# A macaron block on one core: the first and last feed-forward tiles in seven block products, and attention values in full-height matmuls

## The chip, the cores and the metric

One core of a Trainium2 chip runs the kernel. It has a matrix engine (TensorE; PE is its matmul side, PEld its weight loads), VectorE (DVE), ScalarE (ACT), GpSimd (POOL) and SyncE (SP), which issues all DMAs here. The metric is device time in microseconds (us) of one execution, lower is better; a kernel's time is the median of its runs.

## The reference

`x` is 4 sequences of 256 tokens with 512 features, all in fp32. Three steps are added one after the other, each on the layer norm of `x` (mean and variance, no gain):

```python
x = x + 0.5 * ffn(_layernorm(x))
x = x + attn(_layernorm(x))
x = x + 0.5 * ffn(_layernorm(x))

def ffn(x):                          # same weights both times; xf is 1024 x 512
    probs = softmax(xf @ W_router.T)             # 8 experts, the best two kept and renormalized -> w
    h = einsum('td,erd->ter', xf, lora_A)        # rank 16 for each expert
    lora_out = einsum('ter,eor,te->to', h, lora_B, w) * 2.0
    return xf @ W_base.T + b_base + lora_out     # W_base is 512 x 512

def attn(x):                         # 32 query heads, 8 key/value heads, head size 128, rotary positions
    # a query sees itself and the 127 tokens before it
    return softmax(mask(q @ k.T / sqrt(128))) @ v @ wo
```

## The kernel before, in words

The 1024 tokens are 8 tiles of 128 tokens (`xt[0..7]`, in SBUF throughout), in two halves of two sequences each. The first feed-forward step (`f1`) goes by halves, the attention by units (half, group of four query heads, sequence; 32 units), the second feed-forward step (`f2`) by sequences, that is, by pairs of tiles.

**Feed-forward.** `ffn(tiles, tag, then)` returns a function that runs one step by its letter and a tile or pair number: M measures a tile (mean, variance and, on ACT, the root), X scales it, T transposes it (PE, then a copy by ACT), N is X and T, A multiplies by the router and the low-rank weights, R is the router (some 16 small DVE operations in a chain and one Exp on ACT, then POOL scales the low-rank activations), G transposes those and ACT copies them (`ht`), I adds the halved bias to `x` on POOL, and L multiplies `ht` by `lb_sb`, adds the bank times 0.5 to `xt` and calls `then` (which stores a tile or measures it for the attention).

The product with `W_base` comes in two forms. The plain one is B (L352 to 357): per tile four matmuls of 512 columns; for the last tile of all, H and K do it by halves of columns (L438 to 448). The other takes a pair of tiles as a 2x2 matrix of blocks (tokens by features), as is `W_base`, and makes seven products in place of eight: S forms the sums of token blocks on POOL (`sums_a`: s1, s2, s4 and a21 in place, in this order), W those of the weight on DVE (`sums_b`: t3, t1, t2, t4), and each product is two matmuls of 256 columns. P makes products 1 and 6, Q makes 5 and 7, C makes 2 and 3, D makes 4. P and Q also combine their banks on DVE (and one ACT copy); Y adds the rest to `xt` on POOL. In the kernel before, the first pair of `f1` and both pairs of the last half's `f2` are plain, the others by seven products.

**Values.** For each unit `values` (L747 to 777) multiplies the transposed probabilities by v. Its queries are eight blocks of 32 (times four heads); blocks 0 to 3 see the first 128 keys (`p0`), blocks 4 to 7 see parts of the first 128 (`old_p`) and of the second (`new_p`). The kernel makes four matmuls of 128 rows by 256 columns and four of 64 rows by 128 columns, the latter in turn on the lower and the upper 64 rows, into two PSUM banks (`oa`, `ob`) in an order of blocks of its own, which three ACT copies undo into `oT`.

**Order.** POOL and ACT run in the written order throughout. PE and DVE do so until three units before the end (`in_order.close()`), after which the framework orders them. The head is a written list of steps, shared by both halves of `f1` and the attention's first steps (`None`); the last units run steps of the second-last sequence's `f2` from the table `loose`; the tail is a list for the last two pairs (`f2[0]`, `f2[1]`) and the last output projection (`None`, 512 columns per matmul, L838). PSUM has four banks for `mm_bank` (products C, D, B, values, projections) and four for `score_bank` (transposes, A, P, Q, scores), each taken in turn.

Of the kernel before, what the change touches and what calls it, by code (L numbers as in the profile page):

```python
# [14 lines left out]
ALU = mybir.AluOpType  # L15
# [23 lines left out]
def macaron_kernel(  # L39
# [21 lines left out]
    def mm_bank(name):  # L61
        return ps.tile([P, 512], F32, tag="mm", bufs=4, name=name)

    def score_bank(name):
        return ps.tile([P, 512], F32, tag="s", bufs=4, name=name)
# [161 lines left out]
    rank = const.tile([P, E], F32, name="rank")  # L227
    for e in range(E):
        nc.gpsimd.memset(rank[:, e : e + 1], float(E - e))
    nc.gpsimd.tensor_scalar(half_bias, half_bias, 0.5, None, ALU.mult)  # L230


    moments = {}
# [13 lines left out]
    def scale(t, tag):  # L247
        if (tag, t) not in moments:
            measure(t, tag)
        mv, std = moments[tag, t]  # L250
        std = std or deviation(t, tag, mv)
        rstd = sb.tile([P, 1], F32, tag="rstd", bufs=4, name=f"rs_{tag}_{t}")
        nc.vector.reciprocal(rstd, std)
        xc = sb.tile([P, D], F32, tag="xc", bufs=3, name=f"xc_{tag}_{t}")
        if tag == "f1":
            shift = sb.tile([P, 1], F32, tag="shift", bufs=4, name=f"sh_{tag}_{t}")
            nc.vector.scalar_tensor_tensor(shift, mv[:, 0:1], -1.0, rstd, ALU.mult, ALU.mult)
            for cols in (slice(0, D // 2), slice(D // 2, D)) if t == 0 else (slice(0, D),):
                nc.scalar.activation(xc[:, cols], xt[t][:, cols], AF.Identity, bias=shift, scale=rstd)
        else:  # L260
            nc.vector.tensor_scalar(xc, xt[t], mv[:, 0:1], rstd, ALU.subtract, ALU.mult)
        moments[tag, t] = xc
# [49 lines left out]
    def ffn(tiles, tag, then):  # L312
# [76 lines left out]
            nc.vector.scalar_tensor_tensor(dst, bank, 0.5, other, ALU.mult, ALU.add)  # L389

        def one_six(j):
            bank = product(j, (1, 6), score_bank(f"p16_{tag}_{tiles[2 * j]}"))
            p1, u2 = temp("p1c", j)[:, lo], temp("u2", j)[:, lo]
            nc.scalar.mul(p1, bank[:, lo], 0.5)
            half_add(u2, bank[:, hi], p1)
            x0 = xt[tiles[2 * j]]
            half_add(x0[:, lo], bank[:, lo], x0[:, lo])
            state[j] = u2

        def seven_five(j):  # L400
            bank = product(j, (7, 5), score_bank(f"p75_{tag}_{tiles[2 * j]}"))
            u = temp("v1", j).rearrange("p (n f) -> p n f", n=2)
            half_add(
                u, bank.rearrange("p (n f) -> p n f", n=2),
                state.pop(j).unsqueeze(1).to_broadcast([P, 2, D // 2]),
            )
            x1 = xt[tiles[2 * j + 1]]
            half_add(x1[:, hi], bank[:, hi], x1[:, hi])
            state[j] = u

        def others(j):
            x0, x1, u = xt[tiles[2 * j]], xt[tiles[2 * j + 1]], state.pop(j)
            for x, n in ((x1[:, lo], 0), (x0[:, hi], 1), (x1[:, hi], 0)):
                nc.gpsimd.tensor_tensor(x, u[:, n], x, ALU.add)

        def two_three(j):
            po[2 * j] = product(j, (2, 3), mm_bank(f"po_{tag}_{tiles[2 * j]}"))

        def four(j):
            po[2 * j + 1] = product(j, (4,), mm_bank(f"po_{tag}_{tiles[2 * j + 1]}"))  # L420
# [9 lines left out]
        def leave(i):  # L430
            bank, t = po.pop(i), tiles[i]
            nc.tensor.matmul(  # L432
                bank, state["ht"][:, i, :], lb_sb, start=False, stop=True, skip_group_check=i // 2 in lhs
            )
            nc.vector.scalar_tensor_tensor(xt[t], bank, 0.5, xt[t], ALU.mult, ALU.add)
            then(t)

        def columns(i, cols):  # L438

            bank, t = mm_bank(f"po_{tag}_{tiles[i]}_{cols.start}"), tiles[i]  # L440
            if cols.start == 0:
                bias(t)
            part, xs = bank[:, : D // 2], xt[t][:, cols]
            for c in range(KC):
                nc.tensor.matmul(part, x_of(i, c), wb_sb[:, c, cols], start=(c == 0), stop=False)
            nc.tensor.matmul(part, state["ht"][:, i, :], lb_sb[:, cols], start=False, stop=True)
            nc.vector.scalar_tensor_tensor(xs, part, 0.5, xs, ALU.mult, ALU.add)
            nc.sync.dma_start(out=out[ts(t, P), cols], in_=xs)

        steps = {  # L450
            "M": look, "X": shape, "T": turn, "N": enter, "A": narrow, "R": shares, "G": gated,
            "S": sums, "I": biases, "P": one_six, "Q": seven_five, "Y": others, "C": two_three, "D": four,
            "B": base, "L": leave, "H": lambda i: columns(i, slice(0, D // 2)),
            "K": lambda i: columns(i, slice(D // 2, D)),
        }
        return lambda s: steps[s[0]](*(int(i) for i in s[1:]))

# [287 lines left out]
        return p0, parts  # L745

    def values(h, g, b, p0, p1):  # L747


        oT = sb.tile([HD, G, S], F32, tag="oT", bufs=4, name=f"oT_{h}_{g}_{b}")  # L750
        cols, half = ts(g % 2, HD), P // 2
        va, vb = (vS[h, g - g % 2][:, 2 * b + n, cols] for n in range(2))
        old_p, new_p = p1
        banks = [mm_bank(f"o{n}_{h}_{g}_{b}").rearrange("p (i c) -> p i c", i=2) for n in "ab"]

        def blocks(part, e, n=2):
            return part[:, e : e + n].rearrange("p e j q -> p (e j q)")

        def product(n, i, lhs, rhs, at=slice(None)):
            nc.tensor.matmul(  # L760
                banks[n][:, i, at], lhs, rhs, start=(i == 0), stop=True, skip_group_check=True
            )

        product(0, 0, va, blocks(p0, 2))
        product(1, 0, va, blocks(p0, 0))
        product(0, 1, va, blocks(old_p, 0))
        product(1, 1, vb, blocks(new_p, 2))
        for e in range(2):
            product(0, 1, vb[:half], blocks(new_p, e, 1)[:half], ts(e, P))
            product(1, 1, va[half:], blocks(old_p, 2 + e, 1)[half:], ts(e, P))  # L770
        blocks_of = oT.rearrange("p j (e q) -> p e j q", q=BLK)
        for e, n, src in ((2, 4, banks[0]), (0, 2, banks[1][:, 0]), (6, 2, banks[1][:, 1])):
            src = src.rearrange("p i c -> p (i c)") if n == 4 else src
            nc.scalar.copy(  # L774
                blocks_of[:, e : e + n], src.rearrange("p (e j q) -> p e j q", j=G, q=BLK)
            )
        return oT

# [107 lines left out]
    def attn(step):  # L886
        if step == "W":
            new = sb.tile([P, 4, 2, D // 2], F32, tag="qT", name="wbs")
            return sum_base(nc.vector, *(new[:, i] for i in range(4)))
        if step == "K":  # L890
            return sum_weights(step.lower(), *groups[0])
        if step[0] == "S":
            if not tokens:
                tokens.update(sum_tokens(0, *(nc.vector,) * 4))
            return tokens[int(step[1:])]()
        t = int(step[1:])
        if step[0] == "X":
            scale(t, "a")
        else:
            norm_attn(t, scaled=True)  # L900

    for h, order in (
# [5 lines left out]
    ):  # L908
        for step in order.split():
            (attn if h is None else halves[h])(step)  # L910
# [32 lines left out]
    def run(queue, n):  # L943
# [5 lines left out]
    loose = {  # L949
# [4 lines left out]
    }  # L954

    def fill(left, place):
# [6 lines left out]
    for u, (h, g, b) in enumerate(units):  # L963
# [4 lines left out]
        if left < 4:  # L968
            normalize(ahead[0], ahead[2])
        fill(left, 0)  # L970
        parts = []

        def turn(at=(h, g, b), pr=ahead[0]):
# [85 lines left out]
            first()  # L1059
        if left > 1:  # L1060
            exponentials(*ahead)
            if left == 2:
                nc.scalar.activation(root, eps, AF.Sqrt)
            if combine:
                combine()
            late.extend(outputs(h, g, b, oT))
# [11 lines left out]
        elif (h, g) == groups[-2] and b == BPH - 1:  # L1078
            late.append(lambda h=h, b=b: add_sums(h, b))
    f2 = [ffn(tiles(last[0], b, 1), "f2", store) for b in range(BPH)]  # L1080
    for n, order in (
        (0, "N0 N1"), (None, 0), (None, 1), (0, "A0 A1 R B0"), (1, "N0"), (0, "B1"),
        (1, "N1 A0 A1 R"), (0, "G L0 L1"), (1, "B0 G H1 L0 K1"),
    ):
        if n is None:
            out_project(*last, order, oT)
        else:
            for step in order.split():
                f2[n](step)
# [46 lines left out]
```

## Time and profile before

| | |
|---|---|
| median of 3 runs | 769.92 us (769.81 to 771.42) |
| the profiled execution | 769.25 us, of which span 767.5 us, granted clock 1.000 |
| PE busy | 759.9 us, 4198 matmul records (an fp32 matmul is two) |
| DVE, POOL, ACT busy | 550.5, 532.3, 214.3 us |
| 0 to 60 us | PE busy 56.95, DVE 41.80, POOL 44.58 us |
| 732.6 to 767.5 us (after the last values) | PE busy 31.53, DVE 15.44, POOL 6.63 us |
| matmuls of values (L760) | 512 records: 256 of 128x256, 256 of 64x128 |

A line of a timeline gives the start, the length, the engine, the line of the code, the operation, its output and inputs with their shapes, how many were merged, and in brackets the idle time ahead of it and what ended it. A record of PE lasts longer than the distance to the next one, since matmuls overlap in the pipeline.

### The profile page before, as it was taken

What the parts mean: (1) busy time and instruction counts of PE and PEld (TensorE: products, weight loads), DVE (VectorE), ACT (ScalarE), POOL (GpSimd) and SP (SyncE); (2) the same over time, 40 slices, a digit from 0 to 9 for tenths busy, and PEclk for the clock granted to TensorE, in tenths of its full rate; (3) what the DMA queues carried; (4) which work ended last, traced back from release to release, by engine and by line L of the source; (5) the groups of instructions that cost most, each with busy time, mean ns of one, the idle gap of its engine ahead of it and who ended that gap; (6) DMA issues with size and microseconds to landing.
All of it is one profiled execution on the core that took longest, in us unless ns stands there. A gap on an engine that the chain in (4) does not pass through costs nothing.

```text
span 767.5 us, 11815 instructions
## 1 busy us (share of the span) xinstructions
PE 759.9 (99%) x4198; PEld 656.4 (86%) x4198; DVE 550.5 (72%) x1332; ACT 214.3 (28%) x784; POOL 532.3 (69%) x579
## 2 busy tenths in 40 slices
PE   8999999999999999999999999999999999999998
PEld 6878888988898888988898889888898889888855
DVE  5787886858675868578667857586867867595963
ACT  5421132422223130322222232222041222223442
POOL 6877775848767585769594788768575959775802
PEclk9999999999999999999999999999999999999999
DMA  8302111304030303012120403030302111010001
GB/s 310 129 1 83 51 60 29 110 1 138 1 111 27 110 29 107 32 56 83 42 96 1 136 3 111 29 110 28 110 28 70 42 55 56 2 55 29 1 28 55
DMA packets 29483, 49.00 MB, mean 64 GB/s; under 512 B 1137, under 2 KB 10353, under 8 KB 29425
## 3 DMA queue, kind: packets, MB, share of 16 engines
q1 hardware_dynamic: 29424, 48.26, 19.0%
q8 instruction: 33, 0.54, 0.3%
q14 instruction: 26, 0.20, 0.1%
HBM read 46.15 MB, written 2.10 MB: 63 GB/s over the span
## 4 chain that ended last, share of the span: by engine, by line
PE 96%; DVE 2%; ACT 1%; DMA 0%; issue 0%; DVEq 0%; ACTq 0%
PE q L521 25%; PE y L796 24%; PE k L578 6%; PE oa L760 6%; PE v L628 6%; PE sb L693 5%; PE sa L679 4%; PE ob L760 4%; PE t L732 4%; PE po_f L357 2%; PE p_f L377 2%; PE pa_f L341 2%; PE po_f L377 2%; PE po_f L432 1%; PE pt_f L270 1%; PE y L838 1%
## 5 line engine op out<-in xcount | busy, mean ns | idle before, releaser
L480 POOL TENSOR_TENSOR qT<-ra_q,rb_q 128x512 f32<-128x512 f32 x64 | 81.4, 1274 | 104.5 <-DVE rb_q L474 104.5
L474 DVE TENSOR_TENSOR rb_q<-q,sin_sb 64x512 f32<-64x512 f32 x128 | 88.0, 688 | 1.7
L736 ACT COPY p<-t 128x512 f32<-128x512 f32 x32 | 18.8, 587 | 210.3 <-PE t L732 210.3
L724 POOL TENSOR_TENSOR probs<-probs,sm 128x512 f32<-128x512 f32 x64 | 65.2, 1041 | 14.8 <-DVE sm L721 13.7
L774 ACT COPY oT<-oa 128x512 f32<-128x512 f32 x32 | 18.8, 586 | 184.9 <-PE ob L760 184.9
L796 PE MATMUL y<-wos,oT 128*128 128x256 f32 x248 | 63.7, 379 | 0.0
L796 PE MATMUL y<-wo,oT 128*128 128x256 f32 x248 | 63.7, 379 | 0.0
L521 PE MATMUL q<-xa,wq 128*128 128x256 f32 x256 | 62.0, 385 | 0.7 <-ACT oT L774 0.7
L796 PE MATMUL y<-wo,oTs 128*128 128x256 f32 x244 | 62.6, 379 | 0.0
L760 PE MATMUL oa<-p,v 128*128 128x256 f32 (+1 forms) x256 | 60.9, 339 | 0.1
L521 PE MATMUL q<-xs,wq 128*128 128x256 f32 x256 | 60.5, 379 | 0.2 <-DVE rb_k L474 0.2
L521 PE MATMUL q<-xs,wqs 128*128 128x256 f32 x256 | 60.5, 379 | 0.0
L760 PE MATMUL ob<-p,v 128*128 128x256 f32 (+1 forms) x256 | 58.7, 338 | 0.0
L472 DVE TENSOR_TENSOR ra_q<-q,cos_sb 128x512 f32<-128x512 f32 x64 | 44.2, 691 | 19.7 <-PE q L521 7.2
L521 PEld LDWEIGHTS q<-xa,wq 128*128 128x128 f32 x256 | 47.2, 190 | 9.0 <-ACT oT L774 0.9
L521 PEld LDWEIGHTS q<-xs,wq 128*128 128x128 f32 x256 | 48.6, 190 | 7.1 <-issue 0.5
L521 PEld LDWEIGHTS q<-xs,wqs 128*128 128x128 f32 x256 | 48.6, 190 | 6.6
L796 PEld LDWEIGHTS y<-wo,oT 128*128 128x128 f32 x248 | 46.6, 190 | 6.0
L796 PEld LDWEIGHTS y<-wo,oTs 128*128 128x128 f32 x244 | 46.4, 190 | 6.3
L760 PEld LDWEIGHTS oa<-p,v 128*128 128x128 f32 (+1 forms) x256 | 39.9, 188 | 13.3 <-issue 10.6
L796 PEld LDWEIGHTS y<-wos,oT 128*128 128x128 f32 x248 | 45.8, 190 | 5.3
L715 ACT ACTIVATE probs<-probs,nm 128x32 f32<-128x32 f32 (+3 forms) x128 | 44.8, 358 | 10.8 <-DVE nm L708 6.0
(220 smaller groups left out, 1808.5 us busy)
## 6 DMA issues: line engine op xcount, KB each, us to landing
wq<-in_wq_dram SPq DMA_DIRECT2D x16, 1024.0 KB, 5.5
wo<-in_wo_dram SPq DMA_DIRECT2D x16, 1024.0 KB, 5.1
wk<-in_wk_dram SPq DMA_DIRECT2D x8, 512.0 KB, 3.5
wv<-in_wv_dram SPq DMA_DIRECT2D x8, 512.0 KB, 3.4
x<-in_x_dram SPq DMA_DIRECT2D x8, 256.0 KB, 6.7
out_dram<-x SPq DMA_DIRECT2D x7, 256.0 KB, 2.0
wb_sb<-in_w_base_dram SPq DMA_DIRECT2D x1, 1024.0 KB, 7.3
ar_sb<-in_w_ar_dram SPq DMA_DIRECT2D x1, 272.0 KB, 4.6
```

The costliest lines, as they stand in the source:

```text
L377: nc.tensor.matmul(bank[:, ts(i, D // 2)], lhs[j][m - 1][:, c, :], weights["bs"][m - 1][:, c, :], start=(m in (1, 5, 2, 4) and c == 0), st ...
L472: nc.vector.tensor_tensor(twice(a), twice(src), angle(cos_sb), ALU.mult)
L474: nc.vector.tensor_tensor(twice(b[o : o + half, :]), twice(src[i : i + half, :]), angle(sin_sb[o : o + half, :]), ALU.mult,)
L480: nc.gpsimd.tensor_tensor(dst, view(a), view(b), ALU.add)
L521: nc.tensor.matmul(bank[:, ts(j, S)], w[:, c, ts(j, HD)], x[:, c, :], start=(new and j == 0 and c == 0), stop=(c == 1), skip_group_check=True,
L578: nc.tensor.matmul(dst, w[n - 1][:, c, :], x[n - 1][:, c, :], start=(start and c == 0), stop=(c == 1), skip_group_check=True,)
L628: nc.tensor.matmul(bank[:, i, :], x[n - 1][:, c, ts(i, P)], w[n - 1][:, c, :], start=(start and i == 0 and c == 0), stop=(c == 1), skip_gr ...
L693: nc.tensor.matmul(pb[:, at : at + P + BLK], q[:, NB + m], k[:, o + m * BLK : o + m * BLK + P + BLK], start=True, stop=True,)
L715: nc.scalar.activation(pr[:, n, :keys_of], src[:, :keys_of], AF.Exp, bias=nm[:, n : n + 1], scale=scale, accum_out=sm[:, n : n + 1],)
L724: nc.gpsimd.tensor_tensor(w, w, sm[:, n : n + NB].unsqueeze(2).to_broadcast([P, NB, P]), ALU.mult)
L760: nc.tensor.matmul(banks[n][:, i, at], lhs, rhs, start=(i == 0), stop=True, skip_group_check=True)
L796: nc.tensor.matmul(py[:, ts(i, D // 2)], lhs[n - 1][:, c, :], weights["os", h, g][n - 1][:, c, :], start=(i == 0 and c == 0), stop=(c == 1 ...
```

## The change

- All pairs of tiles go by seven products. In `f1` the first pair gets S0, the products 1, 2, 6, 5, 7, 3, 4 and Y0; in the tail both pairs do. B, H and K are gone from the orders; the very last tile leaves by F, which multiplies `ht` by `lb_sb` and adds and stores it in two halves of columns.
- P, Q, C, L are cut into smaller steps: V and Z are what P and Q did on DVE; 1, 2, 3, 6 are single products; O and E are L without and with only `then`.
- The head's list is written anew. In it, W follows X3 of the first half, the halved bias (H, formerly in the setup of POOL) follows S0, I1 of the first half stands between S1 and R of the second half, and O0 O1 (the first half's) stand ahead of V0 Z0 of the second.
- X of tiles 0 and 1 is split: DVE scales the first 256 features, ACT the others.
- The Sqrt activation that loads ACT's table ahead of the tail moves from the second-last unit to the last one.
- In the last unit, L0 L1 of the second-last sequence's `f2` move from behind `values` to ahead of it.
- The tail's list is written anew, and PE and DVE follow the written order there too.
- `values` becomes three matmuls of 128 rows by 512 columns in two banks (p0; old and new parts accumulated), and two ACT copies.

```diff
-    nc.gpsimd.tensor_scalar(half_bias, half_bias, 0.5, None, ALU.mult)
...
         if tag == "f1":
...
-            for cols in (slice(0, D // 2), slice(D // 2, D)) if t == 0 else (slice(0, D),):
-                nc.scalar.activation(xc[:, cols], xt[t][:, cols], AF.Identity, bias=shift, scale=rstd)
+            cols = slice(D // 2 if t < 2 else 0, D)
+            if t < 2:
+                lo = slice(0, D // 2)
+                nc.vector.tensor_scalar(xc[:, lo], xt[t][:, lo], mv[:, 0:1], rstd, ALU.subtract, ALU.mult)
+            nc.scalar.activation(xc[:, cols], xt[t][:, cols], AF.Identity, bias=shift, scale=rstd)
...
         def one_six(j):
-            bank = product(j, (1, 6), score_bank(f"p16_{tag}_{tiles[2 * j]}"))
-            p1, u2 = temp("p1c", j)[:, lo], temp("u2", j)[:, lo]
+            one(j)
+            six(j)
+
+        def one(j):
+            state[j] = product(j, (1,), score_bank(f"p16_{tag}_{tiles[2 * j]}"))
+
+        def six(j):
+            bank, p1 = state[j], temp("p1c", j)[:, lo]
+            product(j, (6,), bank[:, hi])
             nc.scalar.mul(p1, bank[:, lo], 0.5)
+            state[j] = bank, p1
+
+        def of_six(j):
+            (bank, p1), u2 = state[j], temp("u2", j)[:, lo]
             half_add(u2, bank[:, hi], p1)
             x0 = xt[tiles[2 * j]]
             half_add(x0[:, lo], bank[:, lo], x0[:, lo])
...
-            then(t)
-
-        def columns(i, cols):
...
+        def leave_by_columns(i):
+
+            bank, t = po.pop(i), tiles[i]
+            for cols in (lo, hi):
+                nc.tensor.matmul(
+                    bank[:, cols], state["ht"][:, i, :], lb_sb[:, cols], start=False, stop=True,
+                    skip_group_check=True,
+                )
+            for cols in (lo, hi):
+                xs = xt[t][:, cols]
+                nc.vector.scalar_tensor_tensor(xs, bank[:, cols], 0.5, xs, ALU.mult, ALU.add)
+                nc.sync.dma_start(out=out[ts(t, P), cols], in_=xs)
...
     def values(h, g, b, p0, p1):
...
+        v = vS[h, g - g % 2]
+        cols = ts(g % 2, HD)
+        for i, parts in enumerate(([p0], p1)):
+            po = mm_bank(f"o{'ab'[i]}_{h}_{g}_{b}")
+            for n, part in enumerate(parts):
+                nc.tensor.matmul(
+                    po, v[:, 2 * b + n, cols], part, start=(n == 0), stop=(n == len(parts) - 1)
+                )
             nc.scalar.copy(
-                blocks_of[:, e : e + n], src.rearrange("p (e j q) -> p e j q", j=G, q=BLK)
+                oT[:, :, ts(i, P)].rearrange("p j (e q) -> p e j q", e=NB),
+                po.rearrange("p (e j q) -> p e j q", e=NB, j=G),
             )
...
     for h, order in (
-        (0, "M0 M1 X0 X1 T0 T1 M2 A0 X2 M3 A1 T2 X3 B0 T3 A2 A3 S1"), (None, "W"), (1, "M0 M1 X0 X1"),
-        (0, "B1 I1"), (1, "T0 T1 M2 M3 X2 X3"), (0, "P1 Q1"), (1, "T2 A0 A1 S0"), (0, "Y1 R C1 D1"),
-        (1, "T3 A2 A3 S1 R P0"), (0, "G"), (1, "Q0"), (0, "L0 L1"), (None, "X0 X1"), (0, "L2 L3"),
-        (1, "C0 D0"), (None, "K X2"), (1, "Y0 P1"), (None, "T0 T1 X3"), (1, "Q1 G C1 L0 D1"),
+        (0, "M0 M1 X0 X1 T0 T1 M2 A0 X2 M3 A1 S0"), (None, "H"), (0, "T2 X3"), (None, "W"),
+        (0, "10 20 T3 60 V0 A2 A3 S1"), (1, "M0 M1"), (0, "Q0"), (1, "X0 X1"), (0, "Z0 30 D0 Y0 I0"),
+        (1, "T0 T1 M2 M3 X2"), (0, "P1 V1"), (1, "X3"), (0, "Q1 Z1"), (1, "T2 A0 A1 S0"),
+        (0, "Y1 R C1 D1"), (1, "T3 A2 A3 S1"), (0, "I1"), (1, "R P0"), (0, "G"), (1, "Q0"), (0, "O0 O1 E0 E1"), (1, "V0 Z0"), (None, "X0 X1"),
+        (0, "L2 L3"), (1, "C0 D0"), (None, "K"), (1, "Y0 P1 V1"), (None, "T0 T1 X2 X3"),
+        (1, "Q1 Z1 G C1 L0 D1"),
         (None, "T2 T3 S1"), (1, "L1"), (None, "S2 S3 S4"),
     ):
...
-        3: ("0P0 0Q0", "0C0 0D0", "0G 0Y0 1X0 1X1"), 2: ("0L0 0L1 1T0 1T1", "1A0 1A1 1S0 1I0", "", "1R"),
-        1: ("1P0 1Q0", "1C0 1D0", "1G 1Y0", "1L0 1L1"),
+        3: ("0P0 0V0 0Q0 0Z0", "0C0 0D0", "0G 0Y0 1X0 1X1"), 2: ("0L0 0L1 1T0 1T1", "1A0 1A1 1S0 1I0", "", "1R"),
+        1: ("1P0 1V0 1Q0 1Z0", "1C0 1D0", "1G 1Y0 1L0 1L1"),
...
+        if left == 1:
+            nc.scalar.activation(root, eps, AF.Sqrt)
...
-            if left == 2:
-                nc.scalar.activation(root, eps, AF.Sqrt)
...
+    ctx.enter_context(
+        tc.manual_schedule(engines={mybir.EngineType.PE, mybir.EngineType.DVE})
+    )
     for n, order in (
-        (0, "N0 N1"), (None, 0), (None, 1), (0, "A0 A1 R B0"), (1, "N0"), (0, "B1"),
-        (1, "N1 A0 A1 R"), (0, "G L0 L1"), (1, "B0 G H1 L0 K1"),
+        (0, "M0 M1 X0 X1 I0"), (None, 0), (0, "T0 T1"), (1, "M0 X0"), (None, 1), (1, "M1 X1 T0"),
+        (0, "A0 A1 S0"), (1, "I0"), (0, "R P0"), (1, "T1"), (0, "Q0 V0 Z0 Y0 C0 D0"), (1, "A0"), (0, "G"),
+        (1, "A1 S0 R"), (0, "L0 L1"), (1, "P0 Q0 V0 Z0 C0 G D0 Y0 L0 F1"),
     ):
```

More of the change, by code (lines that the diff above doesn't have):

```diff
@@ L400, in seven_five, with of_seven @@
         def seven_five(j):
-            bank = product(j, (7, 5), score_bank(f"p75_{tag}_{tiles[2 * j]}"))
+            state["p75", j] = product(j, (7, 5), score_bank(f"p75_{tag}_{tiles[2 * j]}"))
+        def of_seven(j):
+            bank = state.pop(("p75", j))
             u = temp("v1", j).rearrange("p (n f) -> p n f", n=2)
@@ L414, in others, with two, three @@
                 nc.gpsimd.tensor_tensor(x, u[:, n], x, ALU.add)
+        def two(j):
+            po[2 * j] = product(j, (2,), mm_bank(f"po_{tag}_{tiles[2 * j]}"))
+        def three(j):
+            product(j, (3,), po[2 * j][:, hi])
         def two_three(j):
-            po[2 * j] = product(j, (2, 3), mm_bank(f"po_{tag}_{tiles[2 * j]}"))
+            two(j)
+            three(j)
         def four(j):
@@ L435, in leave @@
             nc.vector.scalar_tensor_tensor(xt[t], bank, 0.5, xt[t], ALU.mult, ALU.add)
-            then(t)
-        def columns(i, cols):
[L440 to L448, printed above, removed]
+        def leave_by_columns(i):
[9 more added lines that the diff above has]
+                nc.sync.dma_start(out=out[ts(t, P), cols], in_=xs)
         steps = {
             "M": look, "X": shape, "T": turn, "N": enter, "A": narrow, "R": shares, "G": gated,
-            "S": sums, "I": biases, "P": one_six, "Q": seven_five, "Y": others, "C": two_three, "D": four,
-            "B": base, "L": leave, "H": lambda i: columns(i, slice(0, D // 2)),
-            "K": lambda i: columns(i, slice(D // 2, D)),
+            "1": one, "2": two, "3": three, "6": six, "S": sums, "I": biases, "P": one_six, "V": of_six, "Q": seven_five, "Z": of_seven,
+            "Y": others, "C": two_three, "D": four,
+            "B": base, "L": lambda i: (leave(i), then(tiles[i])), "O": leave,
+            "E": lambda i: then(tiles[i]), "F": leave_by_columns,
         }
@@ L750, in values @@
         oT = sb.tile([HD, G, S], F32, tag="oT", bufs=4, name=f"oT_{h}_{g}_{b}")
[L751 to L773, printed above, removed]
+        v = vS[h, g - g % 2]
[6 more added lines that the diff above has]
+                )
             nc.scalar.copy(
-                blocks_of[:, e : e + n], src.rearrange("p (e j q) -> p e j q", j=G, q=BLK)
+                oT[:, :, ts(i, P)].rearrange("p j (e q) -> p e j q", e=NB),
+                po.rearrange("p (e j q) -> p e j q", e=NB, j=G),
             )
@@ L889, in attn @@
             return sum_base(nc.vector, *(new[:, i] for i in range(4)))
+        if step == "H":
+            return nc.gpsimd.tensor_scalar(half_bias, half_bias, 0.5, None, ALU.mult)
         if step == "K":
```

## The prediction

> **What bounds the kernel now.** I read the page first: the busy line, then the chain that ended last.
>
> ```profile
> PE 759.9 (99%) x4198; PEld 656.4 (86%) x4198; DVE 550.5 (72%) x1332; ACT 214.3 (28%) x784; POOL 532.3 (69%) x579
> ...
> PE 96%; DVE 2%; ACT 1%; DMA 0%; issue 0%; DVEq 0%; ACTq 0%
> ```
>
> TensorE is busy for 99% of the span and is 96% of the chain, at a granted clock of 1.000. So the price of a matmul is the distance to the next start. In the timeline of PE, one record of 256 columns follows the last after 0.216 us, one of 512 after 0.429, one of 128 after 0.111; each fp32 matmul is two records. The stretches then show where PE is not dense: of 0 to 60 us it is busy 56.95, of 732.6 to 767.5 it is busy 31.53, in between nearly always. Next, the timeline of one unit of values:
>
> ```profile
> 305.74 0.59 PE L760 MATMUL ob<-p,v 128*128 128x256 f32 x2
> 306.26 0.37 PE L760 MATMUL oa<-p,v 64*128 64x128 f32 x1
> 306.27 0.37 PE L760 MATMUL ob<-p,v 64*128 64x128 f32 x1
> 306.48 0.27 PE L760 MATMUL oa<-p,v 64*128 64x128 f32 x1
> ...
> 306.91 0.49 PE L628 MATMUL v<-wv,xa 128*128 128x128 f32 x2
> ```
>
> Two half-row records start 0.01 us apart, so a pair costs one. But there are four gaps: the step to half rows costs 0.09 (0.52 from 305.74 to 306.26 instead of 0.43), the first pair lasts 0.21 and the last 0.20 instead of 0.11, and the first full record after them 0.10 more than usual: 0.39 together. Then the waits of PE, and two places of the timeline:
>
> ```profile
> 39.85 1.13 PE L377 MATMUL po_f<-wb_sb,xn_f 128*128 128x256 f32 x4 [0.64 <-DVE x L435]
> 408.63 0.70 PE L521 MATMUL q<-xa,wq 128*128 128x256 f32 x2 [0.67 <-ACT oT L774]
> 751.06 0.63 PE L270 MATMUL pt_f<-ident,xc_f 128*128 128x128 f32 x4 [0.29 <-DVE xc_f L261]
> ```
>
> These are the only waits of over 0.3 us on PE after 12 us that the change touches. Last, DVE beside POOL (timelines of both):
>
> ```profile
> 33.45 0.79 DVE L293 TENSOR_TENSOR s_f<-k_f,r_f 128x32 f32<-128x32 f32 x1
> 33.47 0.73 POOL L121 TENSOR_TENSOR xs_f<-xn_f 128x256 f32<-128x256 f32 x1
> 344.62 1.30 DVE L492 TENSOR_TENSOR xs<-xa,xs 128x512 f32<-128x512 f32 x1
> 345.45 1.60 POOL L126 TENSOR_TENSOR wo<-wo 128x512 f32<-128x512 f32 x1
> ```
>
> A router operation that takes 0.19 with POOL idle takes 0.79 and ends 0.05 after POOL's; a 512-wide subtraction that takes 0.68 alone takes 1.30 and makes POOL's next one 0.33 longer. DVE operations with two SBUF operands and POOL operations alternate; those that read a bank do not (L389 keeps 0.42 beside POOL).
>
> **The change, part by part.** All sums are against the profiled execution: 769.25 us, with a span of 767.5. The median shown is 769.92, 0.67 above it; I add that at the end.
>
> *Products.* A plain pair of tiles is 8 matmuls of 512 columns: 16 records of 0.429, 6.86 us. By seven products it is 28 records of 0.216, 6.05. One pair at the head and two at the end change: 3 x -0.82 = -2.45, all on PE, provided that PE stays dense.
>
> *Values.* A unit now: 2.465 us from its first start to the next instruction's, plus 0.104 on that instruction: 2.569. After: three matmuls of 512 columns, 6 x 0.429 = 2.574. 32 units: +0.2. All units before agree within 0.001 us, so this term is firm. The three ACT copies become two, the first beside the second bank's matmuls. The wait at 408.63 is for bank oa, which its copy frees at 408.58, 0.6 after the unit; after the change that copy is over before the unit ends: -0.7 (0 if it is another bank's).
>
> A rule that speaks against full passes stands in the Trainium skill, "TensorE: Matmul & The Clock Gate", Part 3: matmuls on different row groups run at the same time, 4 ns apart, so the span is that of one. By it alone a unit is 8 x 0.216 + 4 x 0.111 = 2.17 and full passes cost 0.40 x 32 = +12.9 us. The trace has the overlap (0.007 us apart) but also the gaps; "TensorEngine Tiling", Key Properties, says that changing the tiling mode drains the engine, which is what they look like.
>
> *Head.* (a) One of the three pairs: -0.82. (b) wb_sb lands 7.3 us after its issue at 3.19, so about 10.5; the first product can start then instead of at 10.77: -0.2. The split of X0 and X1 between DVE and ACT, and A0 A1 before it, end earlier by some 0.7, but wait for this landing: nothing. (c) Product 6 needs s2 (POOL) and t2, the third subtraction of W (DVE). W, which ran almost alone, now runs beside S0: POOL's setup is through at about 9.1 (half_bias no longer stands in its middle), s2 ends at about 10.6. With the alternation above, DVE's ends are 10.6 + 0.55, POOL's 0.6 after that, and so on: t2 at 13.5. PE has done 1, 2 (1.73) and T3 (0.44) at 12.7: +0.8, between 0 (no alternation) and +1.5 (each waits out the other). A2 and A3 queue behind it. (d) The wait at 39.85 lost 0.79 and 0.10 behind it; it was for bank po of tile 0, freed late because DVE did V0 Z0 ahead of L0. Now O0 O1 come first and PE does L2 L3 meanwhile: -0.9. (e) I1, two POOL additions of 1.27, moves between S1 and the second router; before, that router had POOL quiet from 36.6 on. Each addition can hold one router step: +0.7, between 0 and +1.4; the router, O0 O1, E0 E1, V0 Z0, X0 X1 are one DVE chain up to the attention transposes, so it counts there. V and Z as steps of their own, and H behind S0 on POOL, I cost at nothing: half_bias landed at about 12.15, when S0 ends, and I0 stands some 6 us later; without this cover H's 1.99 would delay S1, which has over 1 us to spare. Sum: -0.4.
>
> *Last three units.* V and Z keep their order. The Sqrt table load (1.28) moves to an ACT that idles; the load at 733.74 goes, under out_project's 3.4 us anyway: 0. L0 L1 now stand ahead of the last values; they can wait up to 0.4 for the copy of ht, or fill the 0.24 for which PE waits for p0 there: 0.
>
> *End.* Two pairs: -1.63. The wait at 750.17 to 751.06 (0.46) goes, since X1 of the last tile is done by 10.5 us after the last values (V) and T1 comes at 11.8: -0.46. I followed the written order with the rows' durations (out_project tile 3.44, T 0.44, A 0.93, two products 1.73, L 0.86): out_project to V+3.4, T0 T1, out_project to 7.8, T0, A0 A1 to 10.1, P0 to 11.8, T1, Q0 C0 D0 to 16.6, A0, G at 17.5, A1, L0 L1 to 20.4, then P0 Q0 C0 G D0 L0 F1 to 28.7. The first router starts at V+10.9 on DVE; two bias additions of POOL (I0 of the last pair) hold it until 13.4, so it ends at 16.3 and POOL's gate at 17.1: 0.4 before G. POOL's Y0 and S0 follow: s2 is 0.2 late for the last P0: +0.2. The second router ends at 24.4 beside those sums; L0 L1 V0 Z0 on DVE then last until 27.4, Y0 on POOL until 29.2, and F1's second half ends at about 29.95, 1.25 behind the last matmul where it is 0.45 now (764.43 to 764.88): +0.8, between 0 and +2. Three stores now leave within 0.8 us, where the one before the last led it by 1.9: +0.2 (0 to 0.6). Sum: -0.9.
>
> Total: -0.4 + 0.2 - 0.7 - 0.9 = -1.8: 767.4 in an execution like the profiled one, 768.1 by the median; I say 768.0.
>
> **The rivals.**
> *All of PE's gain arrives:* c, e and the end's additions are nothing: -2.45 + 0.2 - 0.7 - 0.2 - 0.9 - 0.46 = -4.5, 765.4 by the median. For it: PE is 96% of the chain. Against it: the rows at 33.45 and 344.62.
> *Hidden anyway:* DVE's chains set the norms at the head and the last store, and the products only lengthen PE's waits; what is left is about -0.7 to 0: 769.5. For it: at the head the router chain of DVE already ended last at 39.85.
> *Slower, by POOL against DVE:* the new sums, Y0 and the biases on POOL (21 operations more at the edges, 0.7 us and more each) hold every router. Its place is the first router of the end; the point is its slack of 0.4 at G. If it and the second come 1.5 late each, G waits 1.1 and the last store another 1.5, and with c and e at their upper ends (+0.7, +0.7): -1.8 + 4.0 = +2.2, 772.1. For it: POOL is 69% busy and sits beside each router; against it: in the last 35 us POOL is busy only 6.63. The Trainium skill, "SBUF — State Buffer", "Who interferes with whom", calls the port shared by the two an exclusive lock; where the loser is held for the whole instruction, this is the case that follows, and the 1.30 us row agrees.
> *Slower, by the half rows:* the four gaps are not theirs and stay with full passes, which only add columns: 0.39 x 32 = +12.5 on top of the sum, 780.6. Against it: the gaps have the same length in all 32 units, whatever instruction follows, and stand nowhere else.
> That the new orders don't hold is no case: PE and DVE follow the written order at both edges, and the last units' own order changes only where L0 L1 stand.
>
> **How the numbers follow.** 0.2% is 1.54 us, about what a measurement of this kernel can tell from no change. My forecast, 767 to 769: 0.45, of which 0.32 lies below 768.4 and 0.13 within the bound. All of PE's gain: 0.23. Hidden: 0.14, within. Slower by POOL: 0.15. By the half rows: 0.03. Together faster 0.55, same 0.27, slower 0.18. The range takes in the full gain and the start of the slower case: 765.0 to 771.0.
>
> **What would show it.** Values: six records 0.43 apart in every unit, no 64-row records. Head: DVE's third L126 operation ending at about 13.5 with PE idle before product 6; no wait at the first C0; the second router ending 0.7 later than 37.6, or not. End: no PE wait of over 0.3 after the last values, the last DVE operation over 1 us after the last matmul. I am wrong if a unit of values is not within 0.02 of 2.57, or if PE waits for G at the end.

## The result, and the profile after

768.45 us by the median of 10 runs (767.87 to 769.19), against 769.87 of the kernel before beside it: a ratio of 0.998 (0.997 to 0.9989), or 1.4 us less. The forecast of 768.0 was near, but not for its own reasons: the head, forecast at -0.4, became longer, and the end gave twice what was forecast.

The busy line and the chain that ended last, from the page after:

```profile
PE 756.9 (99%) x3906; PEld 636.1 (83%) x3906; DVE 562.2 (73%) x1346; ACT 211.2 (28%) x750; POOL 548.0 (72%) x600
...
PE 93%; DVE 4%; DMA 1%; ACT 0%; issue 0%; SPq 0%; POOL 0%; POOLq 0%; DVEq 0%; ACTq 0%
```

PE has 3.0 us less to do, and 3 points of the chain have gone from PE, 2 of them to DVE. The stretches after (start and end, length, then busy time and instructions of PE, PEld, DVE, ACT, POOL, then clock, DMA share, GB/s) show where:

```profile
0.00:60.00 60.00, 54.94 (x288) 44.71 (x289) 47.00 (x115) 25.46 (x54) 49.30 (x95) 1.00 0.41 141
...
732.00:766.30 34.30, 30.46 (x140) 21.94 (x138) 23.69 (x65) 7.58 (x20) 16.77 (x22) 0.99 0.13 46
```

In the first 60 us PE is busy 2.0 less than before, of which only 0.8 is work taken out, while DVE has 5.2 and POOL 4.7 more. Another 0.7 is no waiting: the 20 idle matmuls that stand ahead of the first transpose took 3.87 instead of 4.53 in this execution. For the rest PE waits. Its waits after 12 us that are new or have stayed, in its timeline:

```profile
13.76 1.10 PE L379 MATMUL p_f<-wbs,xs_f 128*128 128x256 f32 x4 [0.62 <-DVE wbs L126]
39.74 1.13 PE L379 MATMUL po_f<-wb_sb,xn_f 128*128 128x256 f32 x4 [0.73 <-DVE x L458]
44.73 1.43 PE L272 MATMUL pt_a<-ident,xc_a 128*128 128x128 f32 x8 [0.40 <-DVE rs_a L252]
55.65 1.10 PE L602 MATMUL k<-xs,wks 128*128 128x256 f32 x4 [0.41 <-DVE xs L516]
```

Product 6 of the first pair waits for t2 (0.79 by the distance from the transposes ahead of it), the first C0 for its bank, the attention's transposes for the norms, and product 6 of the keys (L602) for its sums. After 60 us no wait reaches 0.3.

To add up one execution, I cut each trace at four places: the first scores, the first transpose of the last unit's probabilities, PE's last matmul, DVE's last operation. From the span's start to the first scores 77.15 became 78.25; from there to the last transpose 650.58 became 650.03; to the last matmul 36.69 became 34.18; DVE ends 0.84 instead of 0.46 later; the last store closes the span 3.03 instead of 2.62 after that. So +1.1 - 0.55 - 2.5 + 0.4 + 0.4 = -1.2 in the span (767.5 to 766.3). The executions differ by less, 769.25 and 768.43, since 2.10 instead of 1.75 lie outside the span.

### The profile page after: what moved, and what is told of

The parts are those of the page before. It is cut to its first block, busy times and chain, and to the rows that moved or that the text cites. A ratio compares the mean times of both kernels' runs of the same rounds, so it can differ in the third digit from the quotient of the medians.

```text
span 766.3 us, 11215 instructions
## 1 busy us (share of the span) xinstructions
PE 756.9 (99%) x3906; PEld 636.1 (83%) x3906; DVE 562.2 (73%) x1346; ACT 211.2 (28%) x750; POOL 548.0 (72%) x600
## 4 chain that ended last, share of the span: by engine, by line
PE 93%; DVE 4%; DMA 1%; ACT 0%; issue 0%; SPq 0%; POOL 0%; POOLq 0%; DVEq 0%; ACTq 0%
PE q L545 25%; PE y L804 24%; PE ob L778 7%; PE k L602 6%; PE v L652 6%; PE sb L717 5%; PE sa L703 4%; PE oa L778 4%; PE t L756 4%; PE p_f L379 2%; PE po_f L379 2%; PE pa_f L343 2%; PE y L846 1%; PE pt_f L272 1%; PE pv L687 1%; DMA x<-in_x_dram 1%
## 5 line engine op out<-in xcount | busy, mean ns | idle before, releaser
L778 PE MATMUL ob<-p,v 128*128 128x512 f32 x128 | 60.2, 593 | 0.0
L778 PEld LDWEIGHTS ob<-p,v 128*128 128x128 f32 x128 | 24.4, 190 | 30.6 <-issue 22.9
L739 ACT ACTIVATE probs<-sb,nm 128x128 f32<-128x128 f32 x128 | 44.3, 353 | 0.0
```

The costliest lines, as they stand in the source:

```text
L739: nc.scalar.activation(pr[:, n, :keys_of], src[:, :keys_of], AF.Exp, bias=nm[:, n : n + 1], scale=scale, accum_out=sm[:, n : n + 1],)
L778: nc.tensor.matmul(po, v[:, 2 * b + n, cols], part, start=(n == 0), stop=(n == len(parts) - 1))
```

## The experiments

The first router matmul (A) starts between 7.2 and 8.2 us. Part of that is the change: the two kernels without the split of X0 and X1 have it at 8.01 and 8.17, the eight with it at 7.23 to 7.87. So the head below is counted to the first scores in two ways, from A and from the first product with `wb_sb` (10.6 to 11.2 us), the end from the last unit's first transpose to the last matmul; all in us, from one profiled execution each. The second way compares an old head with a new one better, since a kernel that starts A early waits for x2 or `wb_sb` behind it; by it the kernel after and "tail not ordered", which share a head, agree within 0.01. Some scatter is left: before and the values alone share a head too and differ by 0.79, of which 0.55 is one wait for a bank at A1 of the second half (0.82 against 0.27 lost). Where head and time differ, the times decide. Every run had runs of the kernel before beside it, at 769.83 or 769.81.

| kernel | time, runs | ratio to before | head from A | head from the first product | end | DVE behind PE |
|---|---|---|---|---|---|---|
| before | 769.87, 10 | | 69.13 | 66.37 | 36.69 | 0.46 |
| after | 768.45, 10 | 0.998 (0.997 to 0.9989) | 71.02 | 67.52 | 34.18 | 0.84 |
| bias later | 767.49, 8 | 0.9972 (0.9962 to 0.9982) | 70.09 | 66.65 | 34.18 | 0.83 |
| bias in quarters | 767.35, 1 | | 69.75 | 66.38 | | |
| t2 first | 767.40, 1 | | 69.34 | 66.58 | | |
| head as before | 766.78, 5 | 0.9963 (0.995 to 0.9977) | 69.52 | 66.33 | 34.18 | 0.85 |
| values alone | 769.04, 11 | 0.9992 (0.9984 to 1.0001) | 69.92 | 67.15 | 36.50 | 0.46 |
| tail not ordered | 768.89, 10 | 0.9986 (0.9977 to 0.9995) | 70.75 | 67.53 | 34.97 | 0.79 |
| head mended | 765.81, 5 | 0.9945 (0.9933 to 0.9958) | 69.02 | 65.60 | 34.18 | 0.82 |
| Y's order | 765.75, 5 | 0.9943 (0.993 to 0.9957) | 68.40 | 65.40 | 34.18 | 0.86 |

My theory after the result: the head's loss is POOL against DVE. Two additions of the bias (I1) hold the second router, and t2 is third among four subtractions that alternate with POOL's. The rivals: that the head is bound by something the biases only accompany (the landing of `wb_sb`, the banks), and that seven products at the head don't pay at all.

**Bias later.** I1 of the first half goes behind the second router.

```diff
-        (0, "Y1 R C1 D1"), (1, "T3 A2 A3 S1"), (0, "I1"), (1, "R P0"), (0, "G"), (1, "Q0"), (0, "O0 O1 E0 E1"), (1, "V0 Z0"), (None, "X0 X1"),
+        (0, "Y1 R C1 D1"), (1, "T3 A2 A3 S1"), (1, "R P0"), (0, "G"), (1, "Q0"), (0, "I1 O0 O1 E0 E1"), (1, "V0 Z0"), (None, "X0 X1"),
```

> The changed kernel with one step moved: the two bias additions I1 stand after the second router's gating on POOL (ahead of O0) instead of ahead of it. In the changed kernel the second router of the first feed-forward step runs from 32.0 to 39.1 us, with 1.19 and 1.12 us for the steps that meet these additions. Port theory (POOL holds two-operand steps of DVE for its whole instruction, and this chain sets the head): router ends at about 37.3, no PE wait at the first C0 (0.73 now), no wait at the first attention transposes (0.4 now), the keys' product 6 starts at about 54.0 instead of 55.65, and the run is 1.6 us shorter than the changed kernel (some 2.9 below the kernel before). Rival (the loss at the head is PE's wait for W's third subtraction; the router has slack): the router ends earlier, but the keys' product 6 stays within 0.3 of 55.65 and the time is that of the changed kernel.

The second router took 32.81 to 37.81 (5.00) instead of 32.02 to 39.09 (7.07), and the waits at the first C0 and at the attention's transposes went. But a wait at the attention's first query came, so that only 0.9 of the head and 0.96 of the median was gained, not the 1.6 expected. The timeline of this kernel there:

```profile
52.29 3.51 POOL L430 TENSOR_TENSOR x<-v_f,x 128x256 f32<-128x256 f32 x3
...
54.00 1.21 DVE L516 TENSOR_TENSOR xs<-xa 128x512 f32<-128x512 f32 x1
55.14 1.21 DVE L516 TENSOR_TENSOR xs<-xa,xs 128x512 f32<-128x512 f32 x1
...
57.00 1.99 PE L545 MATMUL q<-xa,wq 128*128 128x256 f32 x8 [0.81 <-DVE x L458]
```

Y1 of the second half (L430) now runs beside DVE's sums for the attention, which take 1.21 each, and the L behind them frees the query's bank late. The same collision had moved on.

**Bias in quarters.** The same additions, at the same place, in four pieces of 128 columns.

```diff
-            nc.gpsimd.tensor_tensor(xt[t], xt[t], half_bias, ALU.add)
+            n = 4 if (tag, t) in (("f1", 2), ("f1", 3)) else 1
+            for c in range(n):
+                cols = ts(c, D // n)
+                nc.gpsimd.tensor_tensor(xt[t][:, cols], xt[t][:, cols], half_bias[:, cols], ALU.add)
```

> The changed kernel with each of the two additions of I1 cut into four of 128 columns, in the same place. Port theory, hold by whole instruction: the router steps beside them take at most some 0.5 us instead of 1.19 and 1.12, and the router ends at about 38.0 instead of 39.1 although POOL has as many columns to add. Rival (the two share bandwidth, so that what counts is how long POOL is busy): the steps are slowed for the same 2.5 us in all and the router ends at 39.0 or later.

First the rows of the kernel after, then those of this one:

```profile
34.53 0.76 DVE L300 TENSOR_TENSOR k_f<-k_f,rank 128x32 f32<-128x32 f32 x1
...
35.89 2.49 POOL L353 TENSOR_TENSOR x<-x,half_bias 128x512 f32<-128x512 f32 x2
...
36.02 1.19 DVE L304 TENSOR_TENSOR s_f<-s_f,s_f 128x32 f32<-128x32 f32 x1
37.31 1.12 DVE L305 TENSOR_TENSOR pe_f<-pe_f,s_f 128x32 f32<-128x32 f32 x1
...
38.90 0.19 DVE L308 SCALAR_TENSOR_TENSOR pe_f<-pe_f,den_f 128x32 f32<-128x32 f32 x1
```

```profile
35.45 0.65 DVE L304 TENSOR_TENSOR s_f<-s_f,s_f 128x32 f32<-128x32 f32 x1
...
36.01 3.34 POOL L356 TENSOR_TENSOR x<-x,half_bias 128x128 f32<-128x128 f32 x8
36.20 0.31 DVE L305 TENSOR_TENSOR pe_f<-pe_f,s_f 128x32 f32<-128x32 f32 x1
...
36.98 0.35 DVE L308 SCALAR_TENSOR_TENSOR pe_f<-pe_f,den_f 128x32 f32<-128x32 f32 x1
```

With POOL busy on the same bytes, and for longer (3.34 against 2.49), no router step beside the pieces takes over 0.35, where two beside the whole additions took 1.19 and 1.12. (The step of 0.65 ran beside a sum of 0.72, ahead of the pieces.) So a small step is held for as long as POOL's one instruction lasts, not by POOL's traffic. (The router was through at 37.33, so only the first 1.3 us of the pieces stood beside it.) The Trainium skill, "SBUF — State Buffer", "Who interferes with whom", calls the shared port an exclusive lock; these rows agree. The router took 5.25 (32.08 to 37.33) instead of 7.07, and counted from the first product the head has all of its 1.15 back. Not all of the router's 1.8 is the pieces': 0.6 is the step at 34.53, which in the kernel after met one of POOL's sums (34.52 to 35.24) and here took 0.19.

**t2 first.** DVE makes t1 and t2 ahead of t3 wherever it makes the sums.

```diff
-        for dst, p, q in ((t3, b22, b12), (t1, b12, b11), (t2, b22, t1), (t4, b21, t2)):
+        order = ((t3, b22, b12), (t1, b12, b11), (t2, b22, t1), (t4, b21, t2))
+        if engine is nc.vector:
+            order = (order[1], order[2], order[0], order[3])
+        for dst, p, q in order:
```

> The changed kernel with W's subtractions in the order t1, t2, t3, t4 (t3 first before), nothing else. In the changed kernel W's third result came at 13.61 us, PE waited 0.79 for it, and the first tile of the second half was transposed at 20.00, 12.77 after the first A. Port theory (W alternates with POOL's sums, each operation 1.1): t2 is now second, at about 12.5, the wait falls to at most 0.1, and that distance to 12.0. Since the second router still meets the biases, the keys' product 6 gains the same 0.8 at most. Rival (PE waits there for POOL's s2 or for the bank, not for t2): the wait stays at 0.8.

No wait at product 6 was left; the wait at the first C0 (0.74) and the later ones were. From A the head is 1.7 shorter than after, more than the wait explains, but there A itself stands 0.64 later. From the first product it is 0.94 shorter: the 0.79 of this wait, and 0.15 at the first C0.

**Head as before.** The kernel after with the old head: plain first pair, W behind S1, I1 behind B1, no bias beside the second router.

```diff
-        (0, "M0 M1 X0 X1 T0 T1 M2 A0 X2 M3 A1 S0"), (None, "H"), (0, "T2 X3"), (None, "W"),
...
+        (0, "M0 M1 X0 X1 T0 T1 M2 A0 X2 M3 A1"), (None, "H"), (0, "T2 X3 B0 T3 A2 A3 S1"), (None, "W"), (1, "M0 M1 X0 X1"),
+        (0, "B1 I1"), (1, "T0 T1 M2 M3 X2 X3"), (0, "P1 V1 Q1 Z1"), (1, "T2 A0 A1 S0"), (0, "Y1 R C1 D1"),
...
```

> The changed kernel with the head's list of the kernel before (first pair plain, W after S1, V0 Z0 ahead of L0 L1, I1 early), everything else as changed. If the new head costs what the traces show (keys' product 6 at 55.65 instead of 54.54), the old head brings that product back to 54.5, and the run is 1.1 us shorter than the changed kernel, some 2.5 below the kernel before. Rival (the late start comes from the load of x or from the split of X0 and X1, not from the order): the product stays at 55.3 to 55.7 and the time at that of the changed kernel.

The time is 1.67 below the kernel after, and 3.05 below before. So values and end, with the split of X0 and X1 that stays in, are worth 3.05 together, and the new order of the head takes 1.67 of that back, although it has 0.82 less matmul.

**Values alone**, in the kernel before:

```diff
+            for n, part in enumerate(parts):
+                nc.tensor.matmul(
+                    po, v[:, 2 * b + n, cols], part, start=(n == 0), stop=(n == len(parts) - 1)
+                )
```

> The kernel before with the new values alone (three matmuls of 512 columns, two copies). My sum: a unit takes 2.574 us for 2.569, and the wait of 0.74 at 408.6 goes: 0.5 us shorter in all (0.2 longer to 0.8 shorter). Half-row rival (the gaps of a unit are not owed to its half rows): a unit takes 2.9 and the run is 12 us longer.

The middle was 0.53 shorter than before (650.05 against 650.58), the time 0.8 by medians, with 1.0 just inside the interval. The wait at 408.63 did not stand in it. That is far from the +12.5 of the half-row rival.

**Tail not ordered.** PE and DVE are left to the framework's order in the tail.

```diff
-    ctx.enter_context(
-        tc.manual_schedule(engines={mybir.EngineType.PE, mybir.EngineType.DVE})
-    )
```

> The changed kernel without the written order of PE and DVE in the tail: the framework orders them there as it did in the kernel before. In the changed kernel it is 34.18 us from the last unit's first transpose to the end of the last matmul, and the last DVE operation ends 0.84 later. If the gain of the end is the products' alone (2 x 0.82 and the lost wait for the last X1), this distance stays at 34.2 to 34.5. Rival (the written order brings it, since the framework's order leaves PE waiting for the routers): 35 to 36, and the run is 1 to 2 us longer than the changed kernel.

The end took 34.97, 0.79 more than with the written order, and 0.44 in the medians: above the 34.2 to 34.5 of the first forecast, and short of the rival's 1 to 2 us. PE's waits (what was waited for, then us in total, times, longest) have a line that the kernel after doesn't have:

```profile
PE ph_f L449 <- POOL hl_f L311: 0.3, 1, 0.3
```

This is G of the last pair behind POOL's gate, and by the distances between the matmuls (0.49 ahead of it, 0.30 behind) it is all of the 0.79. DVE does the additions of the first pair's L and two of the last pair's V0 between the steps of the second router there, which ends at 759.53 (757.96 after). The slower rival had named the first router's G; at the second one the written order keeps PE free of a wait.

**Head mended.** Bias later and t2 first together, and Y1 of the second half moved behind L3 of it, away from the sums beside which it stood in "bias later".

```diff
-    halves[1]("Y1")
...
-    for step in "I1 I0".split():
+    for step in "Y1 I1 I0".split():
```

> The changed kernel with three moves at the head: I1 behind the second router, W's t1 and t2 first, and Y1 of the second half behind L3 instead of ahead of the keys (where, with I1 moved, it held two token subtractions of DVE at 1.21 us each and with them the queries, 0.98 us). Port theory: no PE wait before product 6, at the first C0, or at the first query; from the first A to the first scores 70.0 us at most (71.02 in the changed kernel, 70.09 with I1 moved alone, 69.13 in the kernel before), so 0.8 to 2.0 us below the kernel with I1 moved alone, 765.5 to 766.7. Rival (something else is late next, the S and K sums or the bank of L1): no more than 0.4 below it.

765.81: 2.64 below the kernel after and 0.97 below the old head, so the new head as a whole pays once its order is right. How much of the 0.97 is the seven products' isn't shown: no run has the plain first pair with these three moves. PE's two longest waits for sums or weights that are left in its head (what was waited for, then us in total, times, longest):

```profile
PE k L605 <- DVE xs L519: 0.7, 1, 0.7
...
PE p_f L382 <- DMA wb_sb<-in_w_base_dram: 0.5, 1, 0.5
```

**Y's order.** On top of it, Y adds the second columns of the pair's first tile first, which the first of the last L needs.

```diff
-            for x, n in ((x1[:, lo], 0), (x0[:, hi], 1), (x1[:, hi], 0)):
+            for x, n in ((x0[:, hi], 1), (x1[:, lo], 0), (x1[:, hi], 0)):
```

> The same as the kernel with three moves at the head, and Y adds first what the first tile of a pair needs (x0's upper half). At the end of the changed kernel the second-last addition of DVE waits 0.35 us for that operation of POOL after its matmul. If this chain sets the end, the last DVE operation ends 0.3 earlier behind the last matmul (0.5 instead of 0.84) and the run is 0.3 us shorter; rival (DVE's own three additions in a row set it): 0.84 stays.

A miss: DVE still ends 0.86 behind PE. The L before the last is no longer held by POOL (its row now names its own matmul as the last that it waits for), and still only the span's end came 0.2 sooner: DVE's own additions behind the last matmuls set that lag. The time (765.75) can't be told from the 765.81.

## Why the prediction was right or wrong, point by point

**Values: right.** The sum was +0.2 - 0.7 = -0.5; the middle is 0.55 shorter, and 0.53 with this part alone. A unit after, in PE's timeline:

```profile
305.60 1.02 PE L778 MATMUL oa<-p,v 128*128 128x512 f32 x2
306.46 1.88 PE L778 MATMUL ob<-p,v 128*128 128x512 f32 x4
308.18 1.05 PE L652 MATMUL v<-wv,xa 128*128 128x128 f32 x8
```

2.58 from the first start to the next instruction's, against the 2.574 worked out. The four gaps did belong to the half rows: what they cost was all that the half rows saved.

**Head (a), the pair: right on PE**, as the records went. **(b), the landing: wrong by 0.16.** The first product stands at 10.73, not 10.57, right behind x2's transposes, which start at 10.02 after waiting 0.67 for ACT's scaling. **(c), product 6: right.** 0.79 was lost, and t2 ended at 13.61 where the alternation gave 13.5:

```profile
10.80 1.13 POOL L121 TENSOR_TENSOR xs_f<-xn_f,xs_f 128x256 f32<-128x256 f32 x1
11.89 1.17 POOL L121 TENSOR_TENSOR xn_f<-xn_f 128x256 f32<-128x256 f32 x1
...
12.51 2.12 DVE L126 TENSOR_TENSOR wbs<-wb_sb,wbs 128x512 f32<-128x512 f32 x2
```

With t2 as the second subtraction it ended at 12.6 ("t2 first"), ahead of its product: this loss came from the order of four instructions.

**(d) and (e): the steps that failed.** (d) took the wait at the first C0 as gone, since O0 O1 stand ahead of V0 Z0. But O0 and O1 stand behind the router on DVE, and (e) makes the router late: it ended at 39.09, 1.5 later than before instead of 0.7, and the wait stayed: 0.89 and 0.10 behind it, where it had been 0.79 and 0.10. My middle value was half of the upper bound; the two steps took 1.19 and 1.12, nearly as long as the two additions together (2.49). I had named the chain (router, O0 O1, E0 E1, V0 Z0, X0 X1) and charged the delay once, at its end, while I had used an undelayed O0 to strike out the wait at its middle. The upper bound for (e), +1.4, was near the true value, and with it the -0.9 of (d) was not to be had. "Bias later" shows both at once: router 5.00, no wait at C0. The wait at 44.73 is where (e) had put its delay: by the distances it lost 0.96 (0.57 ahead of the transposes, 0.39 among them), for the 0.7. The wait at 55.65 was in no step of the sum; it lost 0.26 more than before. It doesn't follow the bias alone: it is 0.17 in "bias later" and 0.71 in the mended kernel.

So, from the first product on: -0.82 of work, +0.87 at product 6 (0.79, and 0.08 behind it), +0.1 at C0, +0.96 at the transposes, +0.26 at the keys, and -0.27 for a wait at A1 of the second half, which the kernel after doesn't have: +1.1, where 1.15 was measured. Of the 1.5 by which the head missed its -0.4, 1.0 is (d).

**End: right in sign, half in size.** Forecast for PE were -1.63 - 0.46 + 0.2 = -1.9; it was -2.5. The s2 wait of 0.2 did not come, and two gaps of 0.09 to 0.10 between matmuls of the old order (in the rows at 733.50 and 756.19) are gone with it; the last 0.2 I can't place. The first router went as worked out, two steps held, and G without a wait:

```profile
744.51 2.68 POOL L353 TENSOR_TENSOR x<-x,half_bias 128x512 f32<-128x512 f32 x2
...
744.97 1.03 DVE L290 TENSOR_TENSOR l_f<-hl_f,m_f 128x16 f32<-128x16 f32 x1
746.04 1.19 DVE L293 SCALAR_TENSOR_TENSOR k_f<-l_f,rank 128x16 f32<-128x16 f32 x1
...
750.13 0.76 POOL L311 TENSOR_TENSOR hl_f<-hl_f,pe_f 128x128 f32<-128x128 f32 x2 [2.93 <-DVE pe_f L308]
...
751.45 0.38 PE L449 MATMUL ph_f<-ident,hl_f 128*128 128x128 f32 x2
```

The gate ends at 750.9 and G starts at 751.45: a slack of 0.5 where I had 0.4. DVE's lag behind the last matmul grew by 0.4 where I had 0.8, and the span's end lies 0.4 further behind it where I had 0.2. So "over 1 us after the last matmul" was wrong (0.84):

```profile
761.44 1.03 PE L464 MATMUL po_f<-lb_sb,ht_f 128*128 128x256 f32 x4
761.95 0.69 DVE L458 SCALAR_TENSOR_TENSOR x<-po_f,x 128x512 f32<-128x512 f32 x1 [1.19 <-POOL x L430]
762.55 0.75 DVE L470 SCALAR_TENSOR_TENSOR x<-po_f,x 128x256 f32<-128x256 f32 x2
763.09 0.89 SPq L471 DMA_DIRECT2D out_dram<-x  x2
```

**The sum.** Head +1.1 instead of -0.4, values as forecast, end -1.7 instead of -0.9, and 0.35 outside the span: -0.8 instead of -1.8 for these two executions. The median's 0.67 that I added had no ground for the kernel after, whose profiled execution stands at its median; it made up for most of the miss. That 768.0 came so near is luck.

**The rivals.** "All of PE's gain arrives" was not this kernel (-1.4), but with the head mended it nearly is: -4.0 of the -4.5. The slower rival had the mechanism that decided the head, and the wrong place: its point, G's slack at the end, held. "Hidden anyway" fell at the end, where all of the matmul gain arrived. The half rows fell.

**Open.** The 0.35 outside the span: 1.9 to 2.1 us lie there in all kernels with the new head's order, 1.7 to 1.75 in those with the old one, whatever their tail and values; no row shows why. And the wait of the keys' product 6 (0.7 in the mended kernel, where the first of its sums, at 51.03, takes 1.24 beside POOL's sums for the queries): it wasn't tried.

## What to carry to other kernels

A POOL instruction over two SBUF operands held a small two-operand DVE step for nearly its whole length here (1.19 and 1.12 beside 1.25 each), so don't let one stand beside a chain of short DVE steps that a matmul waits for: move it to where DVE reads PSUM or rests, or cut it into pieces. When you strike out a wait, work out its releaser's new time with every delay that you charge elsewhere in the same sum. And when a bulk operation is moved, look at what it stands beside next: "bias later" gave back part of its gain at the next sums, and that wait went only when POOL's operation beside them was moved too.

## What I had not expected of the hardware

- The same bias in eight pieces kept POOL busy for 3.34 us instead of 2.49, and yet the DVE chain that ran into it was 1.8 faster (5.25 against 7.07), 1.2 of it from its steps beside and behind the bias.
- A unit of full-height matmuls costs the same as one with pairs of 64 rows (2.58 against 2.57): 0.39 of gaps ate what the pairs saved.
- Kernels that start alike have their first router matmul at 7.23 to 7.87, in executions whose first instructions stand within 0.03 us of each other. Where the eight transposes ahead of it took 1.33 or 1.34 it stands at 7.23 to 7.45, where they took 1.56 to 1.67 at 7.62 to 7.80; the latest, 7.87, is that of "t2 first", where the second tile of `x` came only at 4.74. Why the transposes differ isn't shown. So distances, not starts, compare two heads.
